# Linear attention of a small vision tower: when a group of tokens is normalised and transposed, and where mixing's first product stands

## The chip, the cores and the metric

The kernel runs on one core of a Trainium2 chip. The metric is the device time of one execution in microseconds (us), and where several runs are shown, their median. The core has five engines that run side by side, each with its own queue of instructions: PE (TensorE, matrix products and transposes), DVE (VectorE), ACT (ScalarE), POOL (GpSimd) and SP, which here only issues DMA transfers.

## The reference, cut to what matters

A tower of two layers works on 128 images with 64 tokens of 256 features each: a tokenizer, a first attention, a feed-forward block of attention experts, then the second layer's linear attention and its experts. The change lies in the linear attention. With `h` of shape (128, 64, 256):

```python
x = layernorm(h)                              # each token of each image
q = to_heads(x @ Wq.T + bq)                   # (1, 8, 64, 128*32), as are k and v
k = to_heads(x @ Wk.T + bk)
v = to_heads(x @ Wv.T + bv)
q = softmax(q, axis=-1)
k = softmax(k, axis=-2)
q = q * sqrt(128*32)
context = einsum('bhnd,bhne->bhde', k, v)
out = einsum('bhnd,bhde->hbne', q, context)   # brought back to (128, 64, 256)
h = h + out
```

`to_heads` makes a head of 8 consecutive tokens times 8 blocks of 32 features, that is of 64 rows; a row's long axis runs over all images and the 32 features of a block. The kernel forms the 64 x 64 products of k and q of a head first, and multiplies v by them.

## The kernel before, in words

The order of every engine's instructions is written out by hand: inside `tc.manual_schedule()` each engine's queue has its instructions in the order in which the Python code emits them. Waits between engines, and on buffers, are put in by the framework. So the order of emission is the schedule.

`linear_attention` (L1388) is a loop of four passes of sixteen steps. Pass n (an object of `Heads`) takes 16 tokens of all images, which is two heads; step i of the pass takes one token. The 64 tokens lie in 16 groups of four (`Group`), group 4n + i // 4 being the one in use at step i. A step emits, in this order (L1838 to L1847):

1. `queries_keys(i)`: four matmuls (two instructions as written, each issued in two parts) of the token's transposed features `xT` with the weights, into one of three PSUM buffers `pp`.
2. `prepare(g, i % 4)`: what gets later groups ready. Statistics of token i % 4 of group g + 3 on DVE; at the fourth step, group g + 3's `factors` on POOL; `normal` of one token of group g + 1 on ACT (L1437, in place); at the fourth step, `transpose` of group g + 1: eight transposes on PE, in two halves of four, each half into one of two PSUM buffers `pt`, and each half copied by ACT to `xT` (L1446, L1447); then the DMA that loads group g + 5.
3. The steps of the list `work` for (n, i), filled by `at(n, i, ...)`. They belong to the pass before this one, or two before.
4. `queries_keys_kept(i)`: DVE adds the bias and moves the PSUM result to the tile `qk` (L1478).
5. In passes 0 to 2, at steps 6, 7, 8, 10, 11, 12, 14 and 15, `values(j)` for two tokens: eight matmul instructions into a `pp` buffer (L1488), and ACT's copy to `v` (L1491).

What `work` holds in passes 1 to 3, for the pass before:

- Steps 0 to 5: `values_transposed`, two at step 0, two at step 1 and one at each of steps 2 to 5. Each is four transposes on PE into a `pt` buffer (L1501) and four ACT instructions that read it (L1504).
- Steps 0 and 1: DVE's `largest`. Step 2: `maximum` (a PE transpose `pm` into the buffer `ps`, L1558, and DVE's `mc` and `dg`, L1561 and L1562), then DVE's `k_max(0)` (L1580). Step 3: `spread` (PE, needs `dg`), `k_max(1)`, and POOL's `k_less` (L1584), which needs `k_max`. DVE's `q_less` (L1570) at steps 4 and 5.
- ACT's exponentials: `k_exp(0)` (L1588) at step 5, ahead of the last `values_transposed`; `q_exp(0)` (L1574) and `k_exp(1)` at step 6; `q_exp(1)` at step 7. DVE's `k_sum` (L1591) at steps 6 and 7, POOL's `k_over_sum` (L1597) at steps 7 and 8.
- Step 10: `scores` (128 small matmuls, L1606) and `scores_kept` (DVE). Step 11: `scores_sums` (two matmul instructions, L1616, then DVE's reciprocal and product on `am`, L1618 and L1619) and at once `mixed(0)` (32 small matmuls of `vT` and `am` into both PSUM buffers `po`, L1628). Steps 12 to 14: `mixed(1)` to `mixed(3)`; `added(k)` (DVE, L1636) a step after `mixed(k)` and ahead of `mixed(k + 1)`, which takes the same two `po` buffers. Step 15: `written`.
- In passes 2 and 3 also, for two passes before: `transposed(k)` at steps 1 to 8 (four transposes into a `pt` buffer, L1650, copied by ACT to `hT`, L1654), and `gates` (L1663) at steps 4 and 8, which read four `hT`.
- At step 11 of pass 3 also, after `mixed(0)`: the load of the last `h`, `maximum_of(0)` (a PE transpose, L1533, then two DVE instructions, L1536 and L1537) and `k_less`.

So the two `pt` buffers serve `values_transposed`, `transposed` and the groups' transposes in turn, each taking the buffer of the one before the last. After the loop, `last` (L1740) ends the attention of the last pass.

Of the kernel before, what the change touches and what calls it, by code (L numbers as in the profile page):

```python
# [1387 lines left out]
def linear_attention(c, front, hd, hx, out, k):  # L1388
# [8 lines left out]
    with (  # L1397
# [282 lines left out]
        work = {}  # L1680

        def at(n, i, f, *a):
            work.setdefault((n, i), []).append(lambda: f(*a))

        for n, x in enumerate(heads[:3]):
            m = n + 1
            for i in range(3):
                at(m, i // 2, x.largest, i)
            at(m, 1, x.largest, 3)
            at(m, 2, x.maximum)  # L1690
            at(m, 2, x.k_max, 0)
            at(m, 3, x.spread)
            at(m, 3, x.k_max, 1)
            for i in range(4):
                at(m, 3 + i // 2, x.k_less, i // 2, i % 2)
                at(m, 4 + i // 2, x.q_less, i)
            for hh in range(2):
                at(m, 5 + hh, x.k_exp, hh)
                at(m, 6 + hh, x.q_exp, hh)
                at(m, 6 + hh, x.k_sum, hh)  # L1700
                at(m, 7 + hh, x.k_over_sum, hh, 0)
                at(m, 7 + hh, x.k_over_sum, hh, 1)
            for k, i in enumerate((0, 0, 1, 1, 2, 3, 4, 5)):
                at(m, i, x.values_transposed, k)
            at(m, 10, x.scores)
            if m == 3:
                at(m, 10, heads[3].k_max, 0)
            at(m, 10, x.scores_kept)
            at(m, 11, x.scores_sums)
            for k in range(4):  # L1710
                at(m, 11 + k, x.mixed, k)
                at(m, 12 + k, x.added, k)
            at(m, 15, x.written)
            if n == 2:
                continue

            for k in range(8):
                at(m + 1, 1 + k, x.transposed, k)
            for k in range(4 if n == 0 else 1):
                at(m + 1, 8 + k, x.moments, 16 * k, 16)  # L1720
            for k in range(2):
                at(m + 1, 4 + 4 * k, x.gates, k)
                at(m + 1, 5 + 4 * k, x.gates_added, k)
# [3 lines left out]
        x = heads[3]  # L1727
# [12 lines left out]
        def last():  # L1740

            x, y, z = heads[3], heads[2], heads[1]
            x.values(0)
            x.largest_of(1)
            x.values(1)
            x.values(2)
            x.maximum_of(1)
            x.k_max(1)
            x.k_less(1, 0)
            x.k_less(1, 1)  # L1750
            x.values(3)
            x.spread_of(1)
            x.q_less_of(1, 0)
            x.values(4)
            x.q_exp_of(1, 0)
            x.q_less_of(1, 1)
            x.values(5)
            x.k_exp_of(1, 0)
            x.q_exp_of(1, 1)
            x.values(6)  # L1760
            x.k_exp_of(1, 1)
            x.values(7)
            x.k_sum(1)
            x.k_over_sum(1, 1)
            x.k_over_sum(1, 0)
            z.moments(16, 32)
            for i in range(2):
                x.values_transposed(i)
            x.scores()
            x.scores_kept()  # L1770
            x.values_transposed(2)
            x.scores_sums()
            x.values_transposed(3)
            z.moments(48, 16)
            for i in range(4):
                x.mixed(i)
                for j in (4 + 2 * i, 5 + 2 * i):
                    if j < 8:
                        x.values_transposed(j)
                if i < 3:  # L1780
                    y.moments(16 * i, 16)
                x.added(i)
            x.written()
            for i in range(4):
                y.transposed(i)
            y.gates(0)
            x.moments(0, 64)
            for i in range(4, 8):
                y.transposed(i)
            y.gates_added(0)  # L1790
            y.gates(1)
            y.moments(48, 16)
            for i in range(4):
                x.transposed(i)
            y.gates_added(1)
            routing.statistics(front.group(0), front.group(1))
            x.gates(0)
            x.gates_added(0)
            for i in range(4, 8):
                x.transposed(i)  # L1800
            x.gates(1)
            x.gates_added(1)

        def prepare(g, i):

            if g + 3 < 16:
                y = groups[g + 3]
                y.statistics(i)
                if i == 3:
                    y.factors()  # L1810
            if g + 1 < 16:
                y = groups[g + 1]
                y.normal(i)
                if i == 3:
                    y.transpose()
            if i == 3 and g + 5 < 16:
                groups[g + 5].load()

        with tc.manual_schedule():
            c.busy(psp.tile([P, 2 * D], F32, tag="pp", name="idle"), w[:, 0], 7)  # L1820
            for g in range(4):
                groups[g].x = front.group(g)
            for g in range(3):
                for i in range(NG):
                    groups[g].statistics(i)
                    if g == 0 and i % 2:
                        groups[0].factors(i - 1, i + 1)
                        for j in range(i - 1, i + 1):
                            groups[0].normal(j)
                if g == 0:  # L1830
                    groups[0].transpose()
                else:
                    groups[g].factors()
            groups[4].load()
            routing.load()
            for n, x in enumerate(heads):
                x.begin()
                for i in range(16):  # L1838
                    x.queries_keys(i)
                    prepare(4 * n + i // NG, i % NG)  # L1840
                    if n < 3 and i == 8:
                        x.load()
                    for step in work.pop((n, i), ()):
                        step()
                    x.queries_keys_kept(i)
                    if n < 3 and i in (6, 7, 8, 10, 11, 12, 14, 15):
                        x.values((6, 7, 8, 10, 11, 12, 14, 15).index(i))  # L1847
            last()
        assert not work

# [379 lines left out]
@with_exitstack  # L2230
def vit_tower(ctx: ExitStack, tc: tile.TileContext, a, out):
    const = ctx.enter_context(tc.tile_pool(name="const", bufs=1))
    dram = ctx.enter_context(tc.tile_pool(name="dram", bufs=1, space=DRAM))
    c = Ctx(tc, const)

    hd = dram.tile([B, T, D], F32, name="hd")

    hx = dram.tile([B, T, D], F32, name="hx")
    gfd = dram.tile([B * T, 1], F32, name="gfd")
    with tc.tile_pool(name="stream", bufs=1) as sp:  # L2240
        c.h2 = sp.tile([P, B // 2, D], F32, name="h2")
        tokenizer(c, a["x"], a["w1"], a["bn1"], a["w2"], a["bn2"])
        front = Front(c, hd, *(a[k] for k in ("wqk1", "bqk1", "wv1", "bv1", "wg")))
        with ExitStack() as rings:
            sh = Shared(c, rings, ExitStack())
            beside, rest = expert_attention(
                c, sh, front, hd, *(a[k] for k in ("normw", "wr", "br", "wqkvf", "wvf", "wproj", "bproj", "wout"))
            )
            rest(*relu_attention(c, sh, a["wqkv0"], a["wmlp"], a["bmlp"], beside))
    c.tables(ctx.enter_context(tc.tile_pool(name="tables", bufs=1)))  # L2250
    with tc.tile_pool(name="gate", bufs=1) as gp:
        k = Routing(c, gp, a["wg"], a["bg"])
        with front.ctx:
            linear_attention(c, front, hd, hx, out, k)
        experts(c, hx, gfd, out, a["we1"], a["we2"], a["be2"], lambda: route(c, k, gfd))
# [71 lines left out]
```

## Time and profile before

| | us |
|---|---|
| runs shown | 2665.02, 2655.38, 2665.51 |
| their median | 2665.02 |
| profiled execution, its own time | 2654.66 |
| its span, first to last instruction | 2652.9 |
| loop of the linear attention, in the span | 1872.9 to 2124.3 |
| pass 1 begins (first `queries_keys`) | 1918.8 |
| pass 2 begins | 1985.7 |
| pass 3 begins | 2059.8 |

The profile is one execution. In the answers quoted below, times count from the first instruction of the span; a line gives start, duration, engine, source line, operation, the tiles written and read, the shape and how many instructions of that kind stand in the line; what stands in brackets is how long the engine had been idle before and whose end released it. PEld is the loading of weights, which overlaps PE. Ends of matmuls are modelled, so two lines of PE may overlap a little.

### The profile page before, as it was taken

Reading aid. Unit: us, or ns where it says so; the run is one execution under the profiler, and the core shown is the slowest. Engines: PE = TensorE matmul, PEld = TensorE weight load, DVE = VectorE, ACT = ScalarE, POOL = GpSimd, SP = SyncE. Lnnn points to the kernel's source line nnn. Section 1 sums busy time; section 2 is a strip of 40 time slices with the busy share of each in tenths; the row PEclk is TensorE's granted clock in tenths of the full one; section 3 lists DMA queues with packets and bytes.
Section 4 is the critical chain, followed back from the end, with each engine's and each line's share of the span. In section 5 each row is a group of like instructions: output and inputs, shape, how many; then the busy total and the mean of one; then the engine's idle time right before and its main releaser. Section 6 shows DMA issues by size and latency. Waiting matters only on the chain. (4 is left out here: it accounts for less than half of the span.)

```text
span 2652.9 us, 81755 instructions
## 1 busy us (share of the span) xinstructions
PE 2526.2 (95%) x35633; PEld 1730.8 (65%) x35633; DVE 2012.2 (76%) x3000; ACT 1623.1 (61%) x3421; POOL 1625.8 (61%) x1428
## 2 busy tenths in 40 slices
PE   8989999999999999899999999999999877999997
PEld 4554444444444444688888888888566556888886
DVE  5759999999999999887878777878467786444443
ACT  2218889899898888666666666666344533233232
POOL 3319989899899999566565666653233313544544
PEclk9999999999999999999999999999999998999998
DMA  3100000000000000000000000000334444555554
GB/s 112 33 13 1 2 2 2 1 2 2 2 2 1 2 13 2 3 28 23 14 23 14 13 24 13 14 23 23 75 73 111 96 128 152 191 185 202 188 189 134
DMA packets 138046, 141.19 MB, mean 53 GB/s; under 512 B 108001, under 2 KB 121859, under 8 KB 129870
## 3 DMA queue, kind: packets, MB, share of 16 engines
q1 hardware_dynamic: 128684, 119.48, 15.3%
q0 software_dynamic: 7648, 14.77, 1.8%
q8 instruction: 281, 4.60, 0.7%
q10 hardware_dynamic: 1344, 1.61, 0.2%
q14 instruction: 89, 0.73, 0.1%
HBM read 104.00 MB, written 32.54 MB: 51 GB/s over the span
## 5 line engine op out<-in xcount | busy, mean ns | idle before, releaser
L540 POOL TENSOR_TENSOR m<-q,k 128x1024 f32<-128x1024 f32 x384 | 719.6, 1907 | 55.9 <-PE sc L342 46.8
L532 DVE TENSOR_TENSOR m<-pc,k 128x2048 f32<-128x2048 f32 (+1 forms) x320 | 646.3, 2055 | 0.5 <-ACT q L472 0.5
L342 PE MATMUL sc<-m,wide 128*32 128x512 f32 x4096 | 520.0, 597 | 8.9 <-ACT m L541 6.6
L541 ACT ACTIVATE m<-m 128x1024 f32<-128x1024 f32 x384 | 402.5, 1049 | 20.4 <-POOL m L540 20.4
L342 PEld LDWEIGHTS sc<-m,wide 128*32 128x32 f32 x4096 | 134.7, 109 | 269.2 <-issue 157.4
L550 ACT ACTIVATE m<-k,q 128x64 f32<-128x64 f32 x1024 | 270.8, 339 | 0.9 <-DVE k L419 0.9
L1070 DVE TENSOR_REDUCE mx<-sc 128x16 f32<-128x1024 f32 x128 | 156.0, 1219 | 133.6 <-PE sc L1058 133.6
L1085 POOL TENSOR_TENSOR e<-e,mx 128x1024 f32<-128x1024 f32 x127 | 241.6, 1903 | 9.9
L1017 ACT COPY kr<-pqk 128x512 f32<-128x512 f32 x254 | 137.9, 604 | 139.3 <-PE pqk L1011 139.3
L2153 PE MATMUL ph<-xt,w1s 128*128 128x256 f32 x896 | 200.5, 382 | 2.2 <-DVE xt L2144 1.5
L2169 PE MATMUL po<-w2s,hT 128*128 128x256 f32 x896 | 198.0, 379 | 0.0
L1084 POOL TENSOR_TENSOR mx<-mx,gate 128x16 f32<-128x16 f32 x127 | 27.4, 216 | 278.3 <-ACT z L1115 162.7
L2153 PEld LDWEIGHTS ph<-xt,w1s 128*128 128x128 f32 x896 | 171.0, 191 | 27.3 <-DVE xt L2144 2.1
L2169 PEld LDWEIGHTS po<-w2s,hT 128*128 128x128 f32 x896 | 168.1, 190 | 21.7
L1097 ACT COPY pT<-pt 128x512 f32<-128x512 f32 x256 | 138.8, 600 | 51.0 <-PE pt L1094 50.8
L1071 DVE TENSOR_TENSOR e<-sc,mx 128x1024 f32<-128x1024 f32 x128 | 156.7, 1224 | 4.4
L2187 POOL DMA_INDIRECT out<-y,rout x56 | 56.6, 1011 | 168.2 <-ACT hT L2157 129.2
L1077 DVE TENSOR_REDUCE mx<-e 128x16 f32<-128x1024 f32 x128 | 152.5, 1191 | 4.0 <-ACT e L1074 3.6
L2157 ACT ACTIVATE hT<-ph,w1s 128x256 f32<-128x256 f32 x224 | 93.0, 470 | 98.6 <-PE ph L2153 95.1
L1094 PE MATMUL pt<-ident,e 128*128 128x128 f32 x1024 | 141.3, 280 | 11.2 <-DVE vr L1047 7.0
L2174 ACT ACTIVATE y<-y,gf 128x256 f32<-128x256 f32 x56 | 28.0, 507 | 195.0 <-issue 110.3
L1074 ACT ACTIVATE e<-e 128x1024 f32<-128x1024 f32 x128 | 139.6, 1091 | 1.2 <-DVE e L1071 1.2
(337 smaller groups left out, 5009.4 us busy)
## 6 DMA issues: line engine op xcount, KB each, us to landing
w1s<-in_we SPq DMA_DIRECT2D x30, 1028.0 KB
w2s<-in_we SPq DMA_DIRECT2D x30, 1024.0 KB
h<-hd SPq DMA_DIRECT2D x4, 2048.0 KB
hx<-h SPq DMA_DIRECT2D x4, 2048.0 KB
out<-h SPq DMA_DIRECT2D x4, 2048.0 KB
xt<-in_x SPq DMA_DIRECT2D x15, 512.0 KB
hd<-h SPq DMA_DIRECT2D x15, 512.0 KB
x<-hd SPq DMA_DIRECT2D x12, 512.0 KB
```

The source lines that it names most:

```text
L342: nc.tensor.matmul(dst[j : j + 32], wide[:, hf, s : s + 32], part, start=start, stop=stop)
L532: nc.vector.tensor_tensor(m, bcast(self.pq[:, hf, i : i + n], 3, T), k, ALU.max)
L540: nc.gpsimd.tensor_tensor(m, bcast(self.q[:, hf, s : s + 2], 3, T), k, ALU.subtract)
L541: nc.scalar.activation(m, m, AF.Relu)
L550: nc.scalar.activation(self.parts[i, hf][:, q], self.blk.k[:, hf, i], AF.Relu, bias=self.q[:, hf, i - NB // 2, q : q + 1], scale=-1.0,)
L1070: nc.vector.tensor_reduce(mx, sc, AX.X, ALU.max)
L1071: nc.vector.tensor_sub(e, sc, bcast(mx, 2, T))
L1077: nc.vector.tensor_reduce(self.sm[x], self.e[x], AX.X, ALU.add)
L1085: eng.tensor_mul(e, e, bcast(sm, 2, T))
L1094: nc.tensor.transpose(pt[:, cq, :], e[:, i : i + 2, :].rearrange("p e s -> p (e s)"), c.ident)
L2153: nc.tensor.matmul(ph[:, j], self.w1[:, w0 : w0 + P], self.xt[:, fc], start=(fc == 0), stop=(fc == 1))
L2169: nc.tensor.matmul(po, self.hT[:, f, r * P : r * P + P], self.w2[:, f, :], start=(f == 0), stop=(f == 7))
```

## The change

Two orders of emission are changed; no instruction is added or taken away.

In `prepare`, the four tokens of group g + 1 are normalised in the first two steps of a group, two in each, where it was one in each of the four; the group's eight transposes and two copies are emitted in the third step, where it was the fourth. The statistics, `factors` and the load of group g + 5 stay where they were, the load in the fourth step.

In the list, `mixed(0)` gets the place 11.5, and the loop now takes up places i + 0.5 at the end of step i. So it is emitted after step 11's `queries_keys_kept` and `values`, and in pass 3 also after `maximum_of(0)` and `k_less`.

```diff
             for k in range(4):
-                at(m, 11 + k, x.mixed, k)
+                at(m, 11 + k if k else 11.5, x.mixed, k)
                 at(m, 12 + k, x.added, k)
...
             if g + 1 < 16:
                 y = groups[g + 1]
-                y.normal(i)
-                if i == 3:
+                if i < 2:
+                    y.normal(2 * i)
+                    y.normal(2 * i + 1)
+                elif i == 2:
                     y.transpose()
             if i == 3 and g + 5 < 16:
                 groups[g + 5].load()
...
                     x.queries_keys_kept(i)
                     if n < 3 and i in (6, 7, 8, 10, 11, 12, 14, 15):
                         x.values((6, 7, 8, 10, 11, 12, 14, 15).index(i))
+                    for step in work.pop((n, i + 0.5), ()):
+                        step()
             last()
```

## The prediction

> **What bounds the kernel now.** I read the page's busy times first, then each engine's busy time by stretches of the loop, PE's waits, and the timelines of PE, ACT and DVE around each wait. The loop is a tenth of the span.
>
> ```profile
> PE 2526.2 (95%) x35633; PEld 1730.8 (65%) x35633; DVE 2012.2 (76%) x3000; ACT 1623.1 (61%) x3421; POOL 1625.8 (61%) x1428
> ```
>
> By stretches (length, then busy us of PE, PEld, DVE, ACT, POOL), steps 4 to 8 of passes 1, 2 and 3:
>
> ```profile
> 1931.00:1950.00 19.00, 15.41 (x59) 9.39 (x58) 17.30 (x27) 14.24 (x23) 14.13 (x14) 1.00 0.30 77
> 1999.00:2024.00 25.00, 22.01 (x97) 12.61 (x96) 22.92 (x61) 17.86 (x31) 17.68 (x15) 1.00 0.37 100
> 2073.00:2096.00 23.00, 18.99 (x74) 9.10 (x73) 18.05 (x33) 18.37 (x31) 16.16 (x11) 0.93 0.10 26
> ```
>
> PE is the engine that should never stop. It is nearly full elsewhere (34.09 of 35 us between 1950 and 1985), and idle some 3 to 4 us in each of these stretches, where DVE is almost as full. PE's waits over the loop (us, times, longest):
>
> ```profile
> PE pt L1446 <- ACT x L1437: 9.9, 7, 4.0
> PE po L1628 <- DVE am L1619: 2.7, 3, 0.9
> PE pq L1474 <- DVE qk L1478: 1.4, 1, 1.4
> PE po L1628 <- DVE h L1636: 1.3, 4, 0.7
> ```
>
> Of the 9.9, 1.3 is the start, before pass 0, unchanged. The rest is three waits at step 7, for the fourth token's normalising (timeline of PE):
>
> ```profile
> 1943.80 0.77 PE L1446 MATMUL pt<-ident,x 128*128 128x128 f32 x5 [1.89 <-ACT x L1437]
> 2014.56 0.77 PE L1446 MATMUL pt<-ident,x 128*128 128x128 f32 x5 [2.75 <-ACT x L1437]
> 2088.47 1.07 PE L1446 MATMUL pt<-ident,x 128*128 128x128 f32 x5 [3.99 <-ACT x L1437]
> 2090.39 2.79 PE L1474 MATMUL pq<-w,xT 128*128 128x512 f32 x4
> ```
>
> ACT's timeline shows why: in pass 1 the token stands behind 3.8 us of exponentials.
>
> ```profile
> 1935.75 1.91 ACT L1588 ACTIVATE qk<-qk 128x2048 f32<-128x2048 f32 x1 [2.06 <-POOL qk L1584]
> 1937.57 1.12 ACT L1504 ACTIVATE vT<-pt,bvs 128x128 f32<-128x128 f32 x4
> 1939.05 1.92 ACT L1574 ACTIVATE qk<-qk 128x2048 f32<-128x2048 f32 x1
> 1940.85 1.92 ACT L1588 ACTIVATE qk<-qk 128x2048 f32<-128x2048 f32 x1
> ...
> 1943.12 0.62 ACT L1437 ACTIVATE x<-x,nb,rs 128x256 f32<-128x256 f32 x1
> ```
>
> But DVE has hardly an idle moment from step 2 to step 7 of pass 1 either. Its chain starts with `maximum`, when PE's `pm` arrives:
>
> ```profile
> 1925.98 0.29 DVE L1561 TENSOR_REDUCE mc<-pm 128x1 f32<-128x128 f32 x1 [0.28 <-PE pm L1558]
> 1994.28 0.29 DVE L1561 TENSOR_REDUCE mc<-pm 128x1 f32<-128x128 f32 x1 [1.57 <-PE pm L1558]
> ```
>
> [...] here two `pt` serve three users, and PE already waits 0.26 us for one in passes 2 and 3. [...] after 3.99 us idle the granted clock was 0.58 up to 2091 and 0.80 up to 2094, and four matmuls took 2.79 instead of 1.88 us; after 2.75 us nothing.
>
> **The change, part by part.** On PE `queries_keys` takes 1.72 us of queue, `values` 1.73, four transposes 0.44, all from starts in the timeline. On ACT a token takes 0.54 (steady), `vT`'s four 1.1, a copy to `xT` 0.54, an exponential 1.85.
>
> *Moved normalising.* Steps 0 and 1 now hold two tokens. At step 0 the second falls into ACT's idle time (0.5 to 1.1 us ahead of `vT`): nothing, or 0.5 without that cover. At step 1 it delays `vT` and the copies by 0.5. In passes 2 and 3 PE's wait for `hT` there grows from 0.26 to 0.77: **0.5 lost each**. In pass 1, PE's new second half of transposes at step 2 waits 0.3 for the fourth `vT`, and 0.1 is saved at step 3: **0.2 lost**. At steps 8 to 15 ACT idles for microseconds, so both tokens are free.
>
> *Moved transposes.* At steps 10 and 14, and in pass 0, two free `pt` buffers and idle ACT hide the move; in pass 0 the 0.24 wait for `xT` at 1881.18 goes: **0.24 won**. At step 2 the eight stand ahead of `maximum`, so `pm` comes 1.2 us later in pass 1 (0.87, and the 0.3 wait), 1.75 in passes 2 and 3 (0.5 + 0.87 + 0.24 for a buffer, and rounding). Queued behind `pm` on DVE: `mc`, `dg`, `k_max`, all `kept`; behind `k_max`, POOL's `k_less`; behind it ACT's `k_exp(0)`; behind that, the last `vT`, whose `pt` buffer the second half of step 6's transposes needs.
>
> Pass 1. POOL's two `k_less` (3.75) end at 36.9 (36.9 stands for 1936.9), so `k_exp(0)` runs 36.95 to 38.85 and the last `vT` to 39.9. PE reaches step 6's transposes at 35.83, does the first half by 36.27, and waits to 40.0: a new wait of 3.7. `values(0)` to 42.2, `queries_keys(7)` to 43.9, `values(1)` at 44.45, when DVE's `kept(6)` has freed its buffer. Before, it started at 44.40. `values(2)` needs `kept(7)`, the end of DVE's full chain: 46.85 + 1.2 = 48.05 against a start at 47.85. So removing 1.89 (and the 1.39 and 0.32 on DVE) brings nothing here: **0.25 lost** for the pass up to there, the 0.2 included.
>
> Pass 2. `queries_keys(6)` 0.5 later, so the transposes come at 07.92 (2007.92), the first half ends at 08.36; ACT had slack: `k_exp(0)` 06.45 to 08.35, last `vT` to 09.4. Wait 1.1. Second half to 9.9, `transposed(5)` 10.4, `values(0)` 12.15, `queries_keys(7)` 13.9, `transposed(6)` 14.35, `values(1)` 16.08. `queries_keys(8)` at 16.1, against 17.79: **1.7 won**, and DVE's `kept(6)` (13.8) and `kept(7)` (17.9) are in time.
>
> Pass 3, in the same way: wait 1.1, `queries_keys(8)` at 87.0 against 90.39 (the slow clock goes too). But `gates(1)` needs the last `hT`, which ACT reaches behind `q_exp(1)` (to 91.4), two tokens (92.4) and its copy (92.95): `gates` ends at 93.4 against 95.32. **1.9 won**.
>
> *mixed(0) moved.* In passes 1 and 2 `values(4)` (1.83) covers the 0.91 that `am` needs: **0.91 won** twice; then `added(0)` (1.28) has only `queries_keys(12)` (1.81) as cover ahead of `mixed(1)`, as `added(2)` has now ahead of `mixed(3)`, without a wait. In pass 3 there are no `values`; `pm` (0.14) goes into the wait, and DVE no longer stands 2.33 us for it, so `added(0)` no longer delays `mixed(1)` (0.22 + 0.19 of the 1.3): **0.6 won**. SP: the load of the last `h` is issued where it was; groups' loads wait for transposes that come earlier.
>
> Sum: 0.24 − 0.25 + 1.7 + 1.9 + 2 × 0.91 + 0.6 = 6.0 won. What follows on PE and DVE is shifted as a whole. The profiled execution, 2654.66, would become 2648.7. Its time lies 10.4 below the median of the runs, 2665.02, and the runs themselves stand at 2655.4 and at 2665; from the median, **2659.0**.
>
> Bounds. If pass 1's new 3.7 us wait slows PE's clock as the 3.99 did, 1.6 more is lost: 4.4 won. If PE's step-6 wait is not there in passes 2 and 3, 2.2 more: 8.2. So by itself this case is 2657 to 2661.
>
> **Rivals.**
>
> A. *The waits simply go.* For it: nothing is added, and ACT idles when the tokens now come. Then 1.89 + 1.39 + 0.32, 2.75 + 0.24, 3.99 and the 1.6 of slow clock, 2.4 for `mixed`, 0.24: 14.8 at most, some 13 with step 1's losses: 2652. Against it: DVE's 17.30 of 19 us in pass 1 and the `pt` queue.
>
> B. *The loop's gain is nil*: DVE's later `pm` binds in passes 2 and 3 as in pass 1, so that 1.7 and 1.9 go and `mixed` only covers the losses: 0 to 2 won, 2664. For it: DVE's 22.92 of 25 us. Against: after `pm` DVE keeps 0.99 and 2.38 us of waits for ACT in front of `k_sum(1)`.
>
> C. *Slower*: step 6's wait for the last `vT`. It is 1.1 us in passes 2 and 3; [...] passes give −1.85, −2.2, −2.0 with 0.24 + 2.4 from the rest: 3.4 lost, 2668.4.
>
> **How the numbers follow.** Chances: forecast 0.55, A 0.15, B 0.2, C 0.1. A measurement of this kernel tells 0.5%, 13.3 us, from no change; the forecast and B lie within it, A at its edge. The runs' two places widen each: a median in the lower place gives 2649 for the forecast, below the edge at 2651.7. Faster: half of A, 0.35 of the forecast, a little of B: 0.28. Slower by over 0.5% needs C and scatter: 0.05. The rest, 0.67, is within. Range 2647 to 2668, from the forecast in the lower place to C; below lies A in the lower place.
>
> **What would show it.** Right: no wait of `pt` for L1437 at step 7; at step 6 waits of L1446 for L1504, about 3.7, 1.1, 1.1; `mc` 1.2 to 1.75 us later; step 11's 0.9 gone in passes 1 and 2; pass 1 about 0.7 us shorter to the start of pass 2, pass 2 about 2.6. Wrong: no wait at step 6 (A), DVE without idle through passes 2 and 3 (B), granted clock below 1 after step 6 in each pass (C).

## The result, and the profile after

| | before | changed |
|---|---|---|
| median, us (20 runs each) | 2661.41 | 2655.63 |
| lowest and highest | 2654.86 to 2669.09 | 2651.66 to 2663.43 |
| ratio changed to before, 95% interval | | 0.9979 (0.9971 to 0.9988) |
| profiled execution, own time | 2654.66 | 2655.06 |
| its span | 2652.9 | 2653.3 |
| loop: pass 0 | 45.84 | 47.03 |
| pass 1 | 66.95 | 67.36 |
| pass 2 | 74.07 | 72.00 |
| pass 3 | 64.52 | 62.59 |
| loop in all | 251.38 | 248.98 |

A pass is measured on PE's timeline from its first `queries_keys` to the next pass's; pass 3 ends at the first `values` after the loop. The runs show 0.21% won, 5.6 us of 2661.4 (3.2 to 7.7 by the interval), inside the 0.5% below which the prediction calls a kernel unchanged. The two profiled executions, by contrast, differ by 0.4 us the other way in their spans, and the loop by 2.4 in favour of the changed kernel: the changed kernel's profile is 4.5 us longer ahead of the loop and 1.7 shorter behind it, where the change alters nothing. A second profile of each, further down, shows how much the loop itself scatters.

Busy times on the page of the changed kernel, as good as those of before:

```profile
PE 2527.0 (95%) x35633; PEld 1731.0 (65%) x35633; DVE 2012.2 (76%) x3000; ACT 1623.9 (61%) x3421; POOL 1627.0 (61%) x1428
```

The same stretches of passes 1, 2 and 3 as shown of before, moved to where the passes now begin (length, busy us of PE, PEld, DVE, ACT, POOL, granted clock, DMA share, GB/s):

```profile
1937.00:1956.00 19.00, 15.48 (x55) 9.86 (x54) 18.04 (x26) 14.43 (x22) 14.03 (x14) 0.91 0.54 102
2005.00:2030.00 25.00, 23.72 (x104) 13.54 (x103) 24.12 (x65) 19.75 (x35) 18.20 (x16) 1.00 0.26 74
2077.00:2100.00 23.00, 19.80 (x81) 9.40 (x80) 20.14 (x38) 18.62 (x32) 16.63 (x12) 1.00 0.13 34
```

PE gets more done in the same time in pass 2 (104 matmuls issued against 97) and pass 3 (81 against 74), less in pass 1 (55 against 59), where the granted clock is 0.91 and was 1.00. PE's waits over the loop, changed kernel (us, times, longest):

```profile
PE pt L1446 <- ACT vT L1504: 5.5, 3, 3.5
PE pg L1663 <- ACT hT L1654: 2.5, 2, 2.2
PE pt L1501 <- ACT hT L1654: 1.5, 2, 0.8
PE pt L1446 <- ACT x L1437: 1.3, 4, 0.7
PE po L1628 <- DVE am L1619: 1.1, 1, 1.1
```

The three waits for the fourth token are gone: what is left for L1437 is the 1.3 us before pass 0. In their place stand three waits at step 6 for the last `vT`, and `gates` now waits for `hT`. On PE's timeline, first pass 1, then pass 2, then pass 3:

```profile
1941.55 0.60 PE L1446 MATMUL pt<-ident,x 128*128 128x128 f32 x4
1945.67 0.92 PE L1446 MATMUL pt<-ident,x 128*128 128x128 f32 x4 [3.52 <-ACT vT L1504]
1946.38 3.36 PE L1488 MATMUL pv<-wvs,xT 128*128 128x256 f32 x8
1949.57 1.88 PE L1474 MATMUL pq<-w,xT 128*128 128x512 f32 x4
1951.34 1.99 PE L1488 MATMUL pv<-wvs,xT 128*128 128x256 f32 x8
...
2015.63 0.66 PE L1446 MATMUL pt<-ident,x 128*128 128x128 f32 x4 [0.98 <-ACT vT L1504]
...
2025.81 1.04 PE L1663 MATMUL pg<-hT,wgs 128*32 128x512 f32 x2 [0.29 <-ACT hT L1654]
...
2087.68 0.66 PE L1446 MATMUL pt<-ident,x 128*128 128x128 f32 x4 [0.98 <-ACT vT L1504]
...
2096.88 1.04 PE L1663 MATMUL pg<-hT,wgs 128*32 128x512 f32 x2 [2.21 <-ACT hT L1654]
```

After 3.52 us idle, `values(0)` took 3.2 us of queue where it took 1.73 before, most of it at half clock (each microsecond from 1946 to 1949 reads 0.50). ACT's timeline of pass 1 shows what the wait was for, and what stands ahead of the copy of the first values:

```profile
1942.67 1.91 ACT L1588 ACTIVATE qk<-qk 128x2048 f32<-128x2048 f32 x1 [2.68 <-POOL qk L1584]
1944.49 1.12 ACT L1504 ACTIVATE vT<-pt,bvs 128x128 f32<-128x128 f32 x4
...
1947.10 1.91 ACT L1574 ACTIVATE qk<-qk 128x2048 f32<-128x2048 f32 x1
1948.91 1.90 ACT L1588 ACTIVATE qk<-qk 128x2048 f32<-128x2048 f32 x1
1950.71 0.58 ACT L1491 COPY v<-pv 128x512 f32<-128x512 f32 x1
```

DVE's `maximum`, in passes 1 and 2:

```profile
1932.90 0.29 DVE L1561 TENSOR_REDUCE mc<-pm 128x1 f32<-128x128 f32 x1 [1.35 <-PE pm L1558]
2002.22 0.29 DVE L1561 TENSOR_REDUCE mc<-pm 128x1 f32<-128x128 f32 x1 [3.37 <-PE pm L1558]
```

Counted from its pass's start it comes 8.43 and 10.39 us in, against 7.21 and 8.56 before: 1.22 and 1.83 later.

### The profile page after: what moved, and what is told of

Same layout as the page of the kernel before. It is cut to its first block, busy times and chain, and to the rows that moved or that the text cites. A ratio compares the mean times of both kernels' runs of the same rounds, so it can differ in the third digit from the quotient of the medians.

```text
span 2653.3 us, 81757 instructions
## 1 busy us (share of the span) xinstructions
PE 2527.0 (95%) x35633; PEld 1731.0 (65%) x35633; DVE 2012.2 (76%) x3000; ACT 1623.9 (61%) x3421; POOL 1627.0 (61%) x1428
```

## The experiments

Edits are against the changed kernel unless said otherwise. Each profile is one execution; ratios are to the kernel before, on the same chip.

### Each half of the change alone

Against the kernel before, `mixed(0)` alone (the loop also takes up places i + 0.5, as in the change):

```diff
-                at(m, 11 + k, x.mixed, k)
+                at(m, 11 + k if k else 11.5, x.mixed, k)
```

> Only mixed(0) is moved behind values(4); tokens and transposes as in the kernel before. Lengths of passes 1, 2 and 3 in the profile, from the first queries_keys of a pass to that of the next (pass 3: to the first values after the loop), were 66.95, 74.07 and 64.52 us before and are 67.36, 72.00 and 62.59 us in the changed kernel. By the forecast's sum: 0.9 won in passes 1 and 2 and 0.6 in pass 3, so 66.0, 73.2 and 63.9, and PE's three waits for the fourth token at step 7 (1.9, 2.7, 4.0 us) stay. In all 2.4 us, ratio 0.999. The rival that the wait for am comes back as a wait of mixed(1) for added(0): 66.9, 74.0, 64.5 and ratio 1.000, with waits of L1628 for L1636 in passes 1 and 2.

Against the changed kernel, `mixed(0)` back in its place, so that only the groups' tokens and transposes are moved:

```diff
-                at(m, 11 + k if k else 11.5, x.mixed, k)
+                at(m, 11 + k, x.mixed, k)
```

> Only the tokens and transposes are moved; mixed(0) stands at step 11 as before. By the forecast the passes are the changed kernel's plus what mixed brings: 68.3, 72.9 and 63.2 us, so pass 1 is longer than before (66.95) and passes 2 and 3 are shorter (74.07, 64.52). PE waits 0.9 us for am at step 11 of each pass. Ratio 0.999, 1 to 4 us won. The rival that the waits at step 7 simply go: all three passes shorter, pass 1 by 1.9 us or more.

Measured: `mixed(0)` alone has passes of 45.84, 66.03, 74.36, 64.08, ratio 0.9993 (0.9985 to 1.0002). Pass 1 is 0.92 shorter, pass 3 0.44. The groups alone: 47.03, 68.44, 74.62, 63.30, ratio 0.9994 (0.9984 to 1.0004). Pass 1 is 1.49 *longer*, pass 3 1.22 shorter. Pass 2 of either profile holds a stretch at half clock (0.50 from 2024 to 2027 with `mixed` alone, from 2044 to 2047 with the groups alone) and can't be read to a microsecond. So `mixed` was worth what the forecast gave it in pass 1 (0.91) and less in pass 3 (0.6), and in pass 1 the groups' part costs 1.49 and not 0.25. Neither half by itself is told from the kernel before.

### `maximum` ahead of the transposes

```diff
+        for m in range(1, 4):
+            at(m, 2, groups[4 * m + 1].transpose)
...
-                elif i == 2:
+                elif i == 2 and (g % 4 or g == 0):
                     y.transpose()
```

At step 2 of passes 1 to 3 the transposes come at the end of the step's list, so `pm` is as early as before the change.

> As the changed kernel, but in step 2 of passes 1 to 3 the eight transposes are emitted at the end of the step's list, behind maximum and the last user of pt there; all else as changed. Theory (a late pm holds DVE's chain, and by k_less and k_exp(0) the wait at step 6 of pass 1): DVE's mc comes 1.2 us or more earlier, the wait at step 6 of pass 1 falls from 3.5 to about 2.3 us, PE's clock does not drop after it, and pass 1 falls from 67.4 to about 65.5 us. In passes 2 and 3 ACT is what k_exp(0) waits for, so the 1.0 us waits at step 6 stay, and the other order at step 2 costs some 0.5 for a pt buffer: 72.5 and 63.1. Rival (pm does not matter, the pt buffer behind the exponential does): pass 1 keeps its 3.5 us wait and 67.4. Rival B of the forecast (DVE's chain binds in all passes): all three passes get shorter by 1 to 2 us.

Measured: 46.75, 65.87, 72.55, 63.13; ratio 0.9982 (0.9974 to 0.9989). `mc` came 7.21 us into pass 1, as before the change, and PE's wait at step 6 fell to 1.62:

```profile
1946.73 0.66 PE L1446 MATMUL pt<-ident,x 128*128 128x128 f32 x4 [1.62 <-ACT vT L1504]
1947.22 1.89 PE L1488 MATMUL pv<-wvs,xT 128*128 128x256 f32 x8
1948.95 1.88 PE L1474 MATMUL pq<-w,xT 128*128 128x512 f32 x4
1952.14 1.99 PE L1488 MATMUL pv<-wvs,xT 128*128 128x256 f32 x8 [1.31 <-ACT v L1491]
```

Two things follow. In passes 2 and 3 an earlier `pm` brought nothing (72.55 and 63.13 against 72.00 and 62.59), so DVE's chain from `pm` doesn't bind there: rival B's mechanism is out. And in pass 1, at full clock (1.00 from 1944 to 1956), `values(1)` waited for ACT's copy of the first values: it starts 25.38 us into the pass, and no sooner because that copy stands behind `q_exp(0)` and `k_exp(1)`.

### The last `vT` ahead of the exponential on ACT

```diff
+            for k, i in enumerate((0, 0, 1, 1, 2, 3, 4, 5)):
+                at(m, i, x.values_transposed, k)
             for hh in range(2):
                 at(m, 5 + hh, x.k_exp, hh)
...
-            for k, i in enumerate((0, 0, 1, 1, 2, 3, 4, 5)):
-                at(m, i, x.values_transposed, k)
```

> As the changed kernel, but at step 5 of passes 1 to 3 ACT's four readings of the last values_transposed are emitted ahead of k_exp(0), where they stood behind it; PE's order is the changed kernel's. Theory (step 6's wait is the pt buffer that ACT holds behind k_exp(0)): the waits of L1446 for L1504 (3.5, 1.0, 1.0 us) are gone in all passes. In pass 1 no clock drop follows, and PE meets DVE's chain instead: 67.4 falls to about 66.2 us. In passes 2 and 3 the copies to xT now stand behind k_exp(0) in the same ACT queue, so transposed(5) waits about 1 us for them and nothing is won: 72.0 and 62.6. Rival (the buffer wait is what costs the time): passes 2 and 3 fall by 1 us each. Rival (DVE's chain alone costs the time in pass 1): pass 1 stays at 67.4.

Measured: 47.03, 65.71, 71.99, 65.65; ratio 0.9977 (0.9969 to 0.9985). PE's waits for `vT` at step 6 are gone. Its timeline in passes 1 and 2:

```profile
1948.56 1.98 PE L1474 MATMUL pq<-w,xT 128*128 128x512 f32 x4 [1.39 <-DVE qk L1478]
1951.72 1.99 PE L1488 MATMUL pv<-wvs,xT 128*128 128x256 f32 x8 [1.18 <-ACT v L1491]
...
2016.47 0.65 PE L1650 MATMUL pt<-ident,h 128*128 128x128 f32 x4 [1.02 <-ACT xT L1447]
```

In pass 2 the wait of 0.98 only changed its name, to 1.02 for `xT` at PE's next transposes, since `xT`'s copies now stand behind the exponential: the pass is the same to 0.01. In pass 1, 1.65 is won, the wait for `v` again being the last. Pass 3 holds two stretches at half clock (0.50 from 2099 to 2102 and from 2123 to 2125) that the changed kernel's pass 3 has not: there it reads 1.00 throughout.

### The wait filled with idle matmuls

The low clock after 3.52 us idle (0.50) was the other candidate for pass 1. Idle matmuls into a `po` buffer, ahead of the second half of step 6's transposes, keep PE busy there: seven in one kernel, four in the other.

```diff
                 for fc in range(2):
+                    if fc and self.g == 6:
+                        c.busy(pso.tile([P, 2 * D], F32, tag="po", name="idle"), w[:, 0], 7)
```

Group 6 is transposed at step 6 of pass 1, so only that place has them; the second kernel has 4 for the 7. It has a second difference, which what was expected does not name: the kernel's own seven idle matmuls, just ahead of the loop, also became four.

```diff
-            c.busy(psp.tile([P, 2 * D], F32, tag="pp", name="idle"), w[:, 0], 7)
+            c.busy(psp.tile([P, 2 * D], F32, tag="pp", name="idle"), w[:, 0], 4)
```

> As the changed kernel, but in pass 1 seven matmuls of 512 columns whose result nobody reads are put between the two halves of step 6's transposes, where PE waited 3.5 us: 3.0 us of work, so 0.5 of wait is left. Nothing that the wait depends on is changed. Separates the wait from the clock. If the half clock after the wait costs its full 1.7 us (forecast's bound), pass 1 falls from 67.4 to about 65.7. If values(1) waits for ACT's copy of values(0), which stands behind q_exp(0) and k_exp(1), only the 0.45 us by which the slow second half delays the copy to xT is won: 66.9. No stretch of half clock from 20 to 25 us after the start of pass 1 in either case. Ratio 0.998.

> The changed kernel with four idle matmuls, eight issues of 0.43 us or 3.44 us, ahead of the second half of step 6's transposes, so that PE's wait for the last vT in pass 1 (3.52 us) is filled, and not lengthened as the 6.0 us of the kernel with seven did. Changed kernel: pass 1 67.36, values(1) at 26.87 us after the pass begins. If the lower clock after the wait costs that pass its full 1.5 us at the end of the pass, pass 1 is 65.9. If values(1) is held by ACT's copy of values(0), which stands behind k_exp(1), then a values(0) that ends 1.5 earlier is copied no earlier (ACT's k_exp(1) ends at 26.0 us either way), values(1) starts where it did and pass 1 is 66.9 to 67.4: then the lower clock cost next to nothing here, and the order of ACT sets the pass. In passes 2 and 3 the idle matmuls fill 1 us of wait and cost some 2.5 us each, so no gain in the whole is expected: ratio 0.998 to 1.000.

Measured with seven: 45.33, 68.22, 72.00, 63.95; ratio 0.9989 (0.9982 to 0.9996). Each idle matmul is issued twice (14 issues for seven), so the filler lasted 6.0 us, not 3.0, and PE reached the second half 2.33 us later than in the changed kernel. Yet the pass grew by only 0.86: the clock stayed full (1.00 all through the pass), and `values(1)`, which here has another buffer, waited for nothing.

Measured with four (3.7 us of PE's queue; the last sentence of what was expected is wrong about the edit, since passes 2 and 3 have no idle matmuls): 46.90, 66.20, 71.99, 63.96; ratio 0.9982 (0.9974 to 0.9989). With fewer idle matmuls ahead of the loop PE waits 2.82 us there for a token, and the clock is at half for 6.8 us (0.50 from 1878 to 1884), in the midst of which pass 0 begins. So pass 0 and the ratio are not the filler's alone; pass 1 lies 47 us on and is read by itself. PE's timeline ahead of the loop and of pass 1, then ACT's copy of the first values:

```profile
1877.77 0.96 PE L1448 MATMUL pt<-ident,x 128*128 128x128 f32 x2 [2.82 <-ACT x L1437]
...
1945.39 3.60 PE L50 MATMUL idle<-w,ident 128*128 128x512 f32 x8
1949.07 0.66 PE L1448 MATMUL pt<-ident,x 128*128 128x128 f32 x4
1949.57 1.89 PE L1490 MATMUL pv<-wvs,xT 128*128 128x256 f32 x8
1951.30 1.88 PE L1476 MATMUL pq<-w,xT 128*128 128x512 f32 x4
1953.58 1.99 PE L1490 MATMUL pv<-wvs,xT 128*128 128x256 f32 x8 [0.40 <-DVE qk L1480]
...
1953.86 0.58 ACT L1493 COPY v<-pv 128x512 f32<-128x512 f32 x1
```

`values(1)` starts 25.71 us into the pass and waits for DVE's `kept(6)`, not for ACT's copy of the first values, which runs only at 1953.86. So in this program it got another of the three `pp` buffers; the programs say the same: the wait that `values(1)` carries names ACT in the changed kernel and in the two experiments above, and DVE in the two filled ones. The kernel with seven has the same buffers without the second difference, so that isn't what changed them. The theory that the copy would hold it back here, 66.9 or more, missed for that reason, and the one of the clock alone, 65.9, was 0.3 short. The run shows what `values(1)` does with `kept(6)`'s buffer and full clock (1.00 throughout pass 1): 25.71, where the forecast had 25.68.

### One number for pass 1

With `mixed(0)` at its new place, or corrected for the 0.92 of it, pass 1 is the start of `values(1)` plus a constant:

| kernel | `values(1)` starts, us into pass 1 | pass 1 | difference |
|---|---|---|---|
| transposes in the fourth step (below) | 24.05 | 64.54 | 40.49 |
| `vT` ahead of the exponential | 25.22 | 65.71 | 40.49 |
| `maximum` first | 25.38 | 65.87 | 40.49 |
| four idle matmuls | 25.71 | 66.20 | 40.49 |
| changed | 26.87 | 67.36 | 40.49 |
| groups alone | 27.03 | 68.44 | 41.41, less 0.92: 40.49 |
| before | 25.63 | 66.95 | 41.32, less 0.92: 40.40 |

The last line is 0.09 lower. So beside `mixed` the change costs the rest of pass 1 only 0.09. Three kernels fall out of the row: that with seven idle matmuls (40.81), and those below with exponentials apart in pass 1 (41.27 with the transposes in the fourth step, 40.38 in the third). There `values(1)` has another buffer, and the waits that follow are others.

### Transposes left in the fourth step, the tokens early

```diff
-                elif i == 2:
+                elif i == 3:
                     y.transpose()
```

> As the changed kernel (tokens normalised two a step, mixed(0) at 11.5), but the group's transposes are back in the fourth step. Tells what the move of the transposes is worth by itself. Theory (in step 2 they hold up pm and at step 6 they meet the pt buffer behind k_exp(0); in the fourth step neither): mc comes as early as before, no wait of L1446 for L1504, the waits for the fourth token stay away. What is late next is ACT: the copies to xT stand behind q_exp(0) and k_exp(1), so transposed(6) at step 7 waits some 1.3 us in pass 2 and 3 us in pass 3. Passes 64.9, 71.8 and 62.4 us against 67.4, 72.0 and 62.6 in the changed kernel (a stretch of PE at half clock adds about 1.7 to a pass). Ratio 0.997. Rival (the third step is what wins, since the fourth stands behind the exponentials): passes 2 and 3 as before less what mixed brings, 73.2 and 63.9.

Measured: 47.28, 64.54, 72.13, 65.59; ratio 0.9975 (0.9966 to 0.9984). The waits for `vT` are gone, and those expected for `xT` came, in passes 2 and 3:

```profile
2018.87 0.66 PE L1650 MATMUL pt<-ident,h 128*128 128x128 f32 x4 [1.71 <-ACT xT L1447]
...
2090.57 0.66 PE L1650 MATMUL pt<-ident,h 128*128 128x128 f32 x4 [2.94 <-ACT xT L1447]
```

Pass 3 holds two stretches at half clock (0.50 from 2110 to 2113 and from 2121 to 2123). So normalising the tokens early, without moving the transposes at all, does as well as the change, as far as these intervals tell.

### Exponentials spread over the steps

With the transposes in the fourth step, the second half's exponentials one step later, so that `xT`'s copies no longer stand behind two of them:

```diff
-                at(m, 5 + hh, x.k_exp, hh)
-                at(m, 6 + hh, x.q_exp, hh)
+                at(m, 5 + 2 * hh, x.k_exp, hh)
+                at(m, 6 + 2 * hh, x.q_exp, hh)
...
-                elif i == 2:
+                elif i == 3:
                     y.transpose()
```

> As the run with the transposes in the fourth step, and ACT's exponentials drawn apart: k_exp(1) goes from step 6 to step 7 and q_exp(1) from step 7 to step 8, so that the copies to xT, the first values and the last hT no longer stand behind them. Theory (once the tokens are early, ACT's order around steps 6 to 8 is what PE waits for, and PE has the room): waits at steps 7 and 8 nearly gone, passes 64.2, 70.5 and 59.7 us, some 11 us under the kernel before in all, ratio 0.996. Rival (DVE's chain is the bound by now: k_sum(1) waits for the later k_exp(1), so kept(7) and POOL's k_over_sum come later, and scores waits for them): passes no shorter than 64.9, 71.8 and 62.4.

Measured: 47.37, 66.21, 70.67, 61.20; ratio 0.9971 (0.9961 to 0.9982). Passes 2 and 3 gain, pass 1 does not, for a wait that was not expected (PE's timeline):

```profile
1947.11 1.98 PE L1474 MATMUL pq<-w,xT 128*128 128x512 f32 x4 [2.80 <-ACT v L1491]
```

`queries_keys(7)` here got the buffer of the first values. The same spread with the transposes in the third step:

```diff
-                at(m, 5 + hh, x.k_exp, hh)
-                at(m, 6 + hh, x.q_exp, hh)
+                at(m, 5 + 2 * hh, x.k_exp, hh)
+                at(m, 6 + 2 * hh, x.q_exp, hh)
```

> As the changed kernel, transposes in the third step, with the exponentials drawn apart in the same way. k_exp(0) stays where it was, so by the theory the waits at step 6 stay (3.5, 1.0, 1.0 us); what goes is the wait of gates(1) at step 8 (0.3 in pass 2, 2.2 in pass 3): passes 67.3, 71.7 and 60.8. Beside the run with the fourth step it shows what the place of the transposes is worth when ACT's order no longer hides it. Rival (the wait at step 6 is cheap): all three passes as short as in that run.

Measured: 45.34, 67.86, 71.44, 66.13; ratio 0.9994 (0.9985 to 1.0003). Pass 1 keeps its 3.5 us wait, and pass 3 holds some 10 us at half clock (0.50 from 2110 to 2115 and from 2123 to 2126), so the 60.8 expected of it can't be tested here. Then the transposes in the fourth step, and the spread in passes 2 and 3 alone:

```diff
-                at(m, 5 + hh, x.k_exp, hh)
-                at(m, 6 + hh, x.q_exp, hh)
+                at(m, 5 + hh * (1 + (m > 1)), x.k_exp, hh)
+                at(m, 6 + hh * (1 + (m > 1)), x.q_exp, hh)
...
-                elif i == 2:
+                elif i == 3:
                     y.transpose()
```

> As the run with the fourth step and the exponentials drawn apart, but in pass 1, where queries_keys(7) then waited 2.8 us for the pp buffer of the first values, the exponentials keep the changed kernel's places. Theory: each pass has its best length of the runs so far, 64.5, 70.7 and 61.2 us, so passes 1 to 3 take 196.4 us against 202.0 in the changed kernel and 205.5 before, each without or with stretches of PE at half clock worth about 1.7. Ratio 0.9965 to the kernel before. Rival (shorter waits only move PE's half-clock stretches elsewhere): passes as expected, but ratio 0.998 and as many stretches as in the changed kernel.

Measured: 47.53, 64.54, 70.66, 64.49; ratio 0.9974 (0.9962 to 0.9986). Passes 1 and 2 are as expected to 0.04, and yet the whole is no better than with the fourth step alone: pass 3 of this profile has two stretches at half clock (0.50 from 2112 to 2114 and from 2122 to 2124), after waits of 1.25 us or less, which is what the expectation's other theory allowed for. The three versions with the transposes in the fourth step beat the kernel before; the one with them in the third is not told from it. Against the changed kernel their intervals overlap its own; none is shown to be better.

### Both kernels once more

> The changed kernel once more, unchanged. If the stretches of half clock (two in its loop, 1.7 us each, one of them ahead of every moved instruction) fall where the execution happens to put them, the one at the loop's start need not come back, and pass 0 is 45.3 without it, 47.0 with it; the one after the 3.52 us wait of pass 1 comes back. If they belong to the program, all come back at the same places: 47.03, 67.36, 72.00, 62.59 within 0.1. The rest of the loop outside such stretches is the same within 0.1 in both cases.

> The kernel before once more, unchanged. If the stretches of half clock fall where the execution happens to put them, one may appear in passes 0 to 2 (45.84, 66.95, 74.07 in the first profile, none of them with one), 1.5 to 1.8 us longer; the one after the 3.99 us wait of pass 3 comes back. If they belong to the program, the four passes are 45.84, 66.95, 74.07 and 64.52 again, within 0.1.

Measured: the changed kernel's passes are 47.03, 67.51, 72.00, 62.58, the same as in its first profile to 0.15, in another execution whose span is 5.5 us longer; ratio 0.9981 (0.9974 to 0.9987). Both of its stretches at half clock came back (0.50 from 1883 to 1886, and from 1952 to 1954 after 3.52 us idle). The kernel before, here a single execution without a ratio, gave 47.27, 66.96, 75.21, 65.45: three passes longer than in its first profile, by 1.43, 1.14 and 0.93. PE's timeline and, in windows (the granted clock follows POOL's busy time), the clock of that second profile of before:

```profile
2021.90 1.33 PE L1446 MATMUL pt<-ident,x 128*128 128x128 f32 x5 [2.76 <-ACT x L1437]
...
2115.16 2.00 PE L1628 MATMUL po<-am,vT 64*128 64x64 f32 x32 [0.91 <-DVE am L1619]
```

```profile
1878.00:1881.60 3.60, 3.47 (x9) 1.57 (x9) 1.14 (x5) 3.10 (x6) 2.08 (x6) 0.55 0.47 119
2021.90:2025.60 3.70, 3.70 (x14) 3.23 (x15) 3.63 (x14) 2.51 (x4) 3.70 (x3) 0.57 0.29 70
2117.20:2120.80 3.60, 3.60 (x7) 1.07 (x6) 2.32 (x5) 0.00 (x0) 0.00 (x0) 0.53 1.38 217
```

The first stretch lies at the loop's start, the second behind the wait of 2.76 us in pass 2 that the change removes, the third shortly after the wait of `mixed(0)`. The same waits left the clock at 1.00 in the first profile. The loop takes 254.89 here and 249.12 in the changed kernel's second profile: 5.77 between them, where the first pair shows 2.40. So the expectation that stretches fall where the execution puts them holds for the kernel before. The two profiles of the changed kernel agree with each other, but two experiments that share its pass 0 ran it without the stretch (45.33 and 45.34), so that one isn't fixed by the program either.

## Why the prediction was right

2659.0 was forecast and 2655.63 measured, within the range, with 6.0 us won forecast and 5.6 measured (3.2 to 7.7). The order of waits is the one forecast, but the close sum is partly luck: the steps made good 3.8 to 4.1 in the profiles (0.24 or 0.5 in pass 0, 0.41 lost in pass 1, 2.07 and 1.93 won in passes 2 and 3), and not 6.0. The 2665.02 that it was taken from also was 3.6 above the later median.

**Pass 0**, 0.24 forecast. Before 45.84 and 47.27 without and with a stretch at half clock at the start; the changed kernel 47.03 with one (0.50 from 1878 to 1881), and 45.33 to 45.34 without in two experiments that differ from it only later. So 0.24 with, 0.5 without. Right.

**The new waits at step 6**, 3.7, 1.1 and 1.1 forecast: 3.52, 0.98 and 0.98. `mc` later by 1.2 and 1.75: 1.22 and 1.83. `k_exp(0)` of pass 1 at 18.18 us into the pass: 18.20. The chain from the transposes over `pm`, DVE, POOL and ACT back to PE is right at every link.

**Pass 1, up to `values(1)`**, 0.25 lost forecast; `values(1)` starts 1.24 later than before, and 1.40 with the groups alone, of whose 1.49 that is most. With `mixed` the pass was to be 0.7 shorter, and it is 0.41 longer. This is the step that failed: "`values(1)` at 44.45, when DVE's `kept(6)` has freed its buffer". In the changed program it has the buffer of the first values, which ACT frees at 1951.29, 26.82 us in, behind `q_exp(0)` and `k_exp(1)`. It starts at 26.87.

That is no new assignment. In the program of the kernel before, too, `values(1)` has the first values' buffer, and ACT's copy stood behind the same two exponentials, just where the dots stand in the prediction's lines of ACT. From the kernel before, ACT's timeline and PE's:

```profile
1942.65 0.59 ACT L1491 COPY v<-pv 128x512 f32<-128x512 f32 x1
1944.40 1.89 PE L1488 MATMUL pv<-wvs,xT 128*128 128x256 f32 x8
```

There the copy ended 24.47 us into the pass, while the fourth token, next in ACT's queue, held PE until 25.03, so nothing waited for the copy. In the changed kernel it ends 2.35 later: `k_exp(0)` is 1.22 later, and ahead of `q_exp(0)` now stand two copies to `xT` in place of one token.

The low clock after the wait (0.50), the bound that the forecast named at 1.6, came too, but it is not a second loss on top: PE, too, was done with the 1.72 us that `queries_keys(7)` takes of its queue only at 1951.29, at that same moment. What each would have cost alone can be estimated from the kernel with four idle matmuls. There, at full clock (1.00), the copy ended 26.57 us into the pass, so `values(1)` could have started at some 26.6 with the first values' buffer. With the other buffer and the low clock, PE would have reached it at some 26.8. Either alone costs most of the 1.24. With `maximum` first the clock was full (1.00) and the copy still held `values(1)` up by 1.31; with four idle matmuls both were out of the way and `values(1)` came at 25.71.

**Pass 2**, 1.7 and 0.91 forecast, 2.07 measured. `queries_keys(8)` starts 30.38 us into the pass, as forecast, 1.69 sooner than before. Then 0.55 is lost around `gates`. The step that failed is "what follows on PE and DVE is shifted as a whole": ACT's last `hT` now stands behind `q_exp(1)` and two tokens, as its timeline of pass 2 shows, and PE waits the 0.29 shown for it.

```profile
2021.89 1.93 ACT L1574 ACTIVATE qk<-qk 128x2048 f32<-128x2048 f32 x1
2023.70 0.59 ACT L1491 COPY v<-pv 128x512 f32<-128x512 f32 x1
2024.17 1.11 ACT L1437 ACTIVATE x<-x,nb,rs 128x256 f32<-128x256 f32 x2
2025.16 0.59 ACT L1654 COPY hT<-pt 128x512 f32<-128x512 f32 x1
```

The forecast worked out just this queue for pass 3 and left it out for pass 2.

**Pass 3**, 1.9 and 0.6 forecast, 1.93 in all measured. `gates` was released 33.05 us in, forecast 33.16; but its last two issues take 0.98 us of queue and the forecast gave them 0.45, so 1.5 was won up to there and not 1.9. `mixed` gave 0.43 (0.44 measured alone), not 0.6: its wait for `am` is still 1.09, so the 0.14 of `pm` only fills what was added to the wait.

**`mixed`** in pass 1: 0.91 forecast, 0.92 measured alone.

**The rivals.** A, the waits simply go: no, three others came. B, nothing won because DVE's later `pm` binds in passes 2 and 3: no, an earlier `pm` makes them no shorter. C, a low clock after step 6 of every pass: it came after the 3.52 us of pass 1 alone (0.50), and after the two waits of 0.98 the clock reads 1.00. That the waits of passes 2 and 3 could bring it too, the profile of before didn't show: C's losses there and its 2668.4 were the author's estimate.

**The rest of the 5.6.** The first pair of profiles shows 2.4 of it in the loop, the second 5.8. The difference is in stretches at half clock of the kernel before, one of them behind a wait that the change removes. Two profiles of each kernel can't show that such stretches make up what the steps leave short, but the mean granted clock is on record, to three digits, for 157 other executions of the kernel before and 40 of the changed one. As an estimate from it, taking all that is missing from 1.00 as time at 0.50, which single microseconds read in the stretches, PE was at half clock for 69.4 us of the whole span on average before and for 65.2 us changed, with an uncertainty of about 1 in the difference. Among the executions of either kernel, each us more at half clock goes with some 0.35 us more time. So these 4.2 us would be worth about 1.5 of the 4.9 us between the mean times of these executions, and 3.4 are left, near what the steps made good. This fits the account; it is a correlation and no experiment.

## What to carry to other kernels

When a wait is taken away, ask of each instruction behind it which buffer it gets, and on which engine's queue that buffer's release stands. Here `values(1)` had the first values' buffer in both kernels. The late copy that frees it was hidden under a wait, and when the wait went and the copy came later still, the copy set the pass. The source doesn't show it; the program's waits do. Where an operation's queue is worked out for one pass, do it for every pass that has it. And a wait moved from one place to another among ACT's exponentials was only renamed (in pass 2, 0.98 us for `vT` became 1.02 for `xT`): having inputs ready early (the tokens) won about as much alone as with their users (the transposes) moved too.

## What the hardware showed

In the loop PE's granted clock falls to half for 3.4 us at a time, and in two kernels for twice as long (6.8 us: four idle matmuls, at the loop's start, and exponentials apart with the transposes in the third step, in pass 3). Single microseconds within the stretches read 0.50, those between them 1.00. Where passes can be compared one stretch costs 0.9 to 1.7 us: 1.43, 1.14 and 0.93 in passes 0, 2 and 3 of the second profile of before against its first, 1.7 in pass 0 of the changed kernel (47.03 with one, 45.33 and 45.34 without in two experiments).

Every gap of 3.50 to 4.00 us on PE in the loop had a stretch at its end: 3.99 and 4.00 in the two profiles of before, 3.99 with `mixed` alone, 3.53 with the groups alone, 3.52 in both profiles of the changed kernel, 3.50 with exponentials apart and the transposes in the third step. But so had one of 2.76 us in the second profile of before and not one of 2.75 in its first, and one of 2.21 us with `vT` ahead of the exponential and in the two filled kernels and not in the changed kernel, while gaps of 2.80 us (exponentials apart, transposes in the fourth step) and 2.94 us (transposes in the fourth step) had none: the clock after them reads 1.00. And pass 3 of four of the kernels above fell to half clock after waits of 1.45 us and less among small matmuls of 64 columns. So the length of a gap alone doesn't tell.

Which of three buffers an instruction gets is laid down in the program, as the releasers of their waits show, and is no fixed rotation. `values(1)` has the first values' buffer in the kernel before, the changed one and six experiments (with `maximum` first it waits 1.31 us for ACT's copy), and `kept(6)`'s in the two with idle matmuls (with four, it waits 0.40 us for DVE), though these matmuls take another kind of buffer. With exponentials apart in pass 1 it has the third one, and `queries_keys(7)` has the first values', for which it waits 2.80 us with the transposes in the fourth step.
